# First feed-forward matrix of a decoder layer: one level of seven products against two levels

## The chip, the cores and the metric

The kernel runs on one core of one Trainium2 chip. A core has a matrix engine (TensorE, called PE, whose weight loads are listed as PEld), a vector engine (VectorE, DVE), an engine for activation functions and copies (ScalarE, ACT), a third elementwise engine (GpSimd, POOL), and SyncE (SP), whose queue issues the DMAs. TensorE writes to PSUM, in eight banks of 128 x 512 single-precision numbers; VectorE and ScalarE read PSUM, GpSimd works in SBUF alone. The metric is the device time in microseconds. Before the change the median of three runs is 2492.58 us (2489.69 to 2492.70).

## The reference

A decoder layer in float32 on x of shape (4, 2048, 512):

```
x = x + _L0_attn_ref(_layernorm(x), ...)            # a linear recurrence over the 4 leading positions
x = x + _L0_xattn_ref(_layernorm(x), ctx_1024, ...) # 16 heads, 77 context rows, softmax
x = x + _L0_ffn_ref(_layernorm(x), ...)
...
h = jnp.einsum('bsd,dh->bsh', x, W_exp) + b_exp     # 512 -> 2048
h = butterfly(h, up_weights, D_HIDDEN)
h = jax.nn.gelu(h + up_bias, approximate=False)
h = butterfly(h, down_weights, D_HIDDEN)
y = jnp.einsum('bsh,hd->bsd', h, W_con) + b_con     # 2048 -> 512
```

W_exp and the first butterfly are both linear, so they are multiplied out once into one matrix of 512 x 2048, the first feed-forward matrix; the second butterfly and W_con become one matrix of 2048 x 512.

## The kernel before

The 2048 positions are cut into 16 units of 128; a unit holds 4 x 128 = 512 rows. First the weight matrices are made (`_prepare`), which takes some 230 us and is mixed with the work of the first units. Then a loop runs over the units.

For each unit `feed_forward` does the two feed-forward products. It also takes a generator `other`, which is `front` of the next unit: layer norm, recurrence (L609), second layer norm, queries (L673), scores (L704), softmax, transposes of the weights (L725), values (L739), output matrix (L673), third layer norm. After each few matmuls of the feed-forward part, `step()` runs `front` to its next `yield`. The order of PE is thus written out by hand: a few feed-forward matmuls, a piece of the next unit's front, and so on. Some yields of `front` issue no PE work; they only let time pass until the norm's statistics and rows are ready (`normed_rows(..., wait, ...)`, 9 such yields ahead of the queries) or until the first softmax is done (4 yields). PE's queue is by hand; the queues of VectorE, ScalarE, GpSimd and SyncE are ordered by the scheduler of the framework, and every engine runs its own queue in order.

The first feed-forward matrix, 512 x 2048 against 512 rows, is done in a seven-product scheme (2 x 2 blocks, seven block products in place of eight). The sums of the left blocks were stored in DRAM as `up7` by `_prepare`; the four sums of the right blocks are made by `combine` (L808 to L811) for each unit. For each of eight output columns `p`, `up` (L838) multiplies a 128 x 128 weight block by 128 x 256 right operands, two matmuls a product, seven products, 56 calls a unit. They accumulate in three PSUM banks; one copy by ScalarE (L854) and five additions by VectorE (L857, L869, L870, L878, L881), all 128 x 256, take them out, and `gelu` (L843) is applied 128 x 256 at a time, spread over the eight columns. The weights come in DMAs of 896 KB (L1072) into a ring of three buffers.

The second matrix is done in 26 products by a list of sums (`DOWN`, `SUMS`, `_down_plan`): sums of activations by GpSimd (`made`, L891), four matmuls a product (L936), additions onto the output by VectorE (L951, L953), weights in DMAs of 512 KB (L930).

TensorE runs a float32 matmul as two records, so that two matmuls stand as four records ("x4") in the timeline.

Of the kernel before, what the change touches and what calls it, by code (L numbers as in the profile page):

```python
# [17 lines left out]
P = 128  # L18
# [7 lines left out]
ORDER = [k + j for j in range(4) for k in (0, NB // 2, NB // 4, 3 * NB // 4)]  # L26
HC = D + 1
PLACE = 2, 0, 6, 1, 3, 4, 5
# [326 lines left out]
def _prepare(nc, keep, pool, room, banks, dram, ident, wexp_t, up_low, up_high, up_bias, dn_low, dn_high, wcon,  # L355
             wup, wdn, low, bias, up7):
# [104 lines left out]
    def plain(i, c, x):  # L461
        for n in range(k):
            nc.sync.dma_start(out=up7[:, :, i, n, :].rearrange("b p q -> p b q"),
                              in_=wup[:, c + n, x : x + h].rearrange("p (b q) -> p b q", q=P))

    plain(PLACE[0], 0, 0)
    for p in range(NB // 2):
        a11, a12, a21, a22 = quarters(p)
        s = spare[:, p % 3 * 1024 : p % 3 * 1024 + 1024].rearrange("p (i k q) -> p i k q", i=4, k=k)
        nc.vector.tensor_tensor(s[:, 0], a21, a22, ALU.add)  # L470
        nc.vector.tensor_tensor(s[:, 2], a11, a21, ALU.subtract)
        nc.gpsimd.tensor_tensor(s[:, 1], s[:, 0], a11, ALU.subtract)
        nc.gpsimd.tensor_tensor(s[:, 3], a12, s[:, 1], ALU.subtract)
        nc.sync.dma_start(out=up7[p][:, 3:7], in_=s)
        if p == NB // 2 - 1:
            plain(PLACE[1], k, 0)
            plain(PLACE[3], k, h)
# [33 lines left out]
def kernel(ctx: ExitStack, tc: tile.TileContext, x, ctx_t, ssm_vec, ssm_vt, ssm_vinv, wq_t, wk_t, wv_t,  # L511
# [75 lines left out]
    def front(u, xt, res, wq=None):  # L587
# [31 lines left out]
        def normed_rows(stats, wait, by_act, last):  # L619
# [14 lines left out]
            for _ in range(wait):  # L634
                yield
# [17 lines left out]
        xnt = yield from normed_rows(second_norm, (1, 12, 9)[min(u, 2)], by_act, False)  # L653
# [66 lines left out]
        def turned(t, g):  # L720
# [6 lines left out]
            if g > 1 or not u:  # L727
                nc.scalar.copy(pt, ps[0:NK])  # L728
            else:
                nc.vector.tensor_copy(pt, ps[0:NK])  # L730
# [22 lines left out]
        for t in range(T + 1):  # L753
# [11 lines left out]
            if t == 2:  # L765
                values(0)
                values(1)
                if u == 1:
                    next_stats()
# [33 lines left out]
    def combine(xnt, res):  # L803


        b11, b12, b21, b22 = (xnt[:, c : c + 2, t : t + 2, :] for c in (0, 2) for t in (0, 2))
        t1, t2, t3, n4 = (tb[:, i].rearrange("p (k t q) -> p k t q", k=2, q=P) for i in range(4))
        nc.vector.tensor_tensor(t1, b12, b11, ALU.subtract)  # L808
        nc.gpsimd.tensor_tensor(t3, b22, b12, ALU.subtract)
        nc.vector.tensor_tensor(t2, b22, t1, ALU.subtract)  # L810
        nc.gpsimd.tensor_tensor(n4, b21, t2, ALU.subtract)  # L811
        res.append((b11, b21, b22, n4, t1, t2, t3))

    def feed_forward(u, xt, rhs, other):
# [19 lines left out]

        def up(p, i, ps, first):
            w = live[p][0][:, PLACE[i - 1]]
# [5 lines left out]
        def gelu(out, x, b):  # L842
# [310 lines left out]
```

## Time and profile before

| | |
|---|---|
| median of three runs | 2492.58 us (2489.69 to 2492.70) |
| profiled execution, its own time | 2492.85 us |
| its span, first to last instruction | 2491.1 us |
| PE busy | 2467.8 us (99%) |
| VectorE busy | 1641.2 us (66%) |
| ScalarE busy | 846.7 us (34%) |
| GpSimd busy | 991.6 us (40%) |
| DMA | 441.26 MB, mean 177 GB/s |
| one unit, from the same matmul in one to that in the next | 147.4 us |

Busy time is the union of the instructions' spans. A matmul record lasts longer than the distance to the next one, since matmuls are pipelined; what a matmul costs PE is read from the distance of starts in the timeline. In the timeline a row merges equal instructions that follow each other: start, length of the whole row, engine, line, names, count, and in brackets how long the engine was idle before and what released it. The unit's length is the distance between rows of the critical chain that recur in each unit (913.78 us and 1061.18 us).

### The profile page before, as it was taken

The numbers are of one execution on the slowest core, as the hardware profiler recorded it, in microseconds if no ns is written. First come the engines' busy times: TensorE is split into PE (matmuls) and PEld (weight loads), VectorE is DVE, ScalarE is ACT, GpSimd is POOL, SyncE is SP. The second block draws the span as 40 slices with busy tenths as digits, with TensorE's granted clock in tenths as the row PEclk, the third lists the DMA queues.
The fourth block names the chain that finished last, engine by engine and source line by source line (L and its number), as shares of the span: only waits on it lengthen the run. The fifth ranks groups of instructions, "written<-read, shape, count | busy, mean of one in ns | idle before, by whom it ended". The sixth has DMA issues, their size and how long they took to land.

```text
span 2491.1 us, 37872 instructions
## 1 busy us (share of the span) xinstructions
PE 2467.8 (99%) x14246; PEld 2139.4 (86%) x14246; DVE 1641.2 (66%) x3843; ACT 846.7 (34%) x1405; POOL 991.6 (40%) x929
## 2 busy tenths in 40 slices
PE   8999999999999999999999999999999999999999
PEld 6877888888888888888888888888888888888888
DVE  6766767576666758667675766767666675765643
ACT  4453234241333414234241423424143341513320
POOL 5534524326152342525235252433515234251534
PEclk9999999999999999999999999999999999999999
DMA  6837554626446362544636355463645646363457
GB/s 215 277 101 287 165 207 144 228 94 207 156 158 218 128 229 98 191 175 151 222 117 225 121 166 190 156 220 103 211 144 161 212 140 221 106 197 139 159 197 250
DMA packets 291427, 441.26 MB, mean 177 GB/s; under 512 B 21049, under 2 KB 247545, under 8 KB 286893
## 3 DMA queue, kind: packets, MB, share of 16 engines
q1 hardware_dynamic: 291246, 438.85, 52.8%
q8 instruction: 114, 1.87, 0.3%
q14 instruction: 67, 0.55, 0.1%
HBM read 398.30 MB, written 39.86 MB: 176 GB/s over the span
## 4 chain that ended last, share of the span: by engine, by line
PE 94%; DVE 2%; DMA 2%; POOL 0%; ACT 0%; issue 0%; SPq 0%; ACTq 0%; POOLq 0%; DVEq 0%
PE ps_a L936 13%; PE ps_b L838 13%; PE ps_b L936 9%; PE ps_a L838 9%; PE ps_c L838 9%; PE ps_w L673 8%; PE ps_q L673 7%; PE ps_c L936 7%; PE ps_sc L704 5%; PE ps_pt L725 4%; PE ps_s L609 3%; PE ps_o L739 2%; PE ps_t L639 2%; PE ps_t L600 1%; PE ps_p L444 1%; DMA arena<-in_up_low 1%
## 5 line engine op out<-in xcount | busy, mean ns | idle before, releaser
L891 POOL TENSOR_TENSOR arena<-arena 128x512 f32<-128x512 f32 x448 | 568.0, 1275 | 533.2 <-ACT arena L843 256.5
L843 ACT ACTIVATE arena<-arena,hbias 128x256 f32<-128x256 f32 x384 | 189.9, 506 | 354.5 <-DVE arena L878 228.7
L838 PE MATMUL ps_b<-arena 128*128 128x256 f32 x1128 | 289.8, 379 | 0.0
L838 PEld LDWEIGHTS ps_b<-arena 128*128 128x128 f32 x1128 | 205.4, 190 | 28.5
L936 PE MATMUL ps_a<-arena 128*128 128x256 f32 x896 | 213.9, 379 | 0.0
L660 POOL TENSOR_TENSOR tq<-tq,xnt 128x512 f32<-128x512 f32 x16 | 20.4, 1272 | 485.6 <-DVE tq L659 470.4
L697 POOL TENSOR_TENSOR pr<-pr,sm 128x616 f32<-128x616 f32 x64 | 104.7, 1636 | 248.9 <-DVE sm L696 183.5
L838 PE MATMUL ps_a<-xnt,arena 128*128 128x256 f32 x752 | 193.2, 379 | 0.0
L936 PE MATMUL ps_b<-arena 128*128 128x256 f32 x768 | 183.8, 379 | 0.0
L936 PEld LDWEIGHTS ps_a<-arena 128*128 128x128 f32 x896 | 165.5, 190 | 20.3 <-DVE xt L951 0.2
L704 PE MATMUL ps_sc<-kbd,qt 128*128 128x308 f32 x480 | 164.7, 425 | 0.6 <-DVE w L557 0.6
L936 PEld LDWEIGHTS ps_b<-arena 128*128 128x128 f32 x768 | 144.7, 190 | 19.0
L936 PE MATMUL ps_a<-w,arena 128*128 128x256 f32 x640 | 159.6, 381 | 0.0
L725 PE MATMUL ps_pt<-ident,pr 128*77 128x128 f32 x1024 | 153.3, 273 | 2.9 <-ACT pt L728 1.5
L838 PEld LDWEIGHTS ps_a<-xnt,arena 128*128 128x128 f32 x752 | 138.4, 190 | 20.2
L673 PE MATMUL ps_q<-xnt,wq 128*128 128x256 f32 x640 | 151.2, 379 | 2.3 <-DMA wq<-wq 2.3
L725 PEld LDWEIGHTS ps_pt<-ident,pr 128*77 128x77 f32 x1024 | 130.4, 148 | 26.6 <-issue 1.9
L707 DVE TENSOR_REDUCE low<-ps_sc 128x4 f32<-128x308 f32 x240 | 114.2, 476 | 52.5 <-PE ps_sc L704 46.4
L673 PEld LDWEIGHTS ps_q<-xnt,wq 128*128 128x128 f32 x640 | 121.2, 190 | 18.9 <-issue 2.7
L628 ACT ACTIVATE xn<-xt,mv,y 128x512 f32<-128x512 f32 x48 | 35.8, 808 | 298.7 <-DVE mv L563 298.7
L936 PEld LDWEIGHTS ps_a<-w,arena 128*128 128x128 f32 x640 | 118.0, 190 | 18.1 <-issue 2.8
L784 DVE TENSOR_TENSOR xt<-ps_w,xt 128x512 f32<-128x512 f32 x99 | 66.3, 688 | 101.0 <-PE ps_w L673 101.0
(225 smaller groups left out, 5035.8 us busy)
## 6 DMA issues: line engine op xcount, KB each, us to landing
arena<-dn SPq DMA_DIRECT2D x256, 512.0 KB, 4.5
w<-dn SPq DMA_DIRECT2D x160, 512.0 KB, 4.0
arena<-up SPq DMA_DIRECT2D x79, 896.0 KB, 4.5
wq<-wq SPq DMA_DIRECT2D x16, 1792.0 KB, 8.9
w<-up SPq DMA_DIRECT2D x32, 896.0 KB, 4.6
xt<-in_x SPq DMA_DIRECT2D x11, 1024.0 KB, 6.3
dn<-arena SPq DMA_DIRECT2D x8, 1152.0 KB, 6.3
out<-xt SPq DMA_DIRECT2D x33, 256.0 KB, 3.3
```

What stands on the lines that cost most here:

```text
L609: nc.tensor.matmul(ps[:, 2 * i : T, f * NS : (f + 1) * NS], lhsT=xpt[:, i, c * (P // NS) + f, :], rhs=gt[:, 0 : T - 2 * i, :], start=i == ...
L639: nc.tensor.transpose(ps[:, c, :], rows[t][:, c * P : (c + 1) * P], ident)
L673: nc.tensor.matmul(tiles[key][:, r, :], lhsT=lhs(i, r, k), rhs=rhs(i, k), start=key == i and r == 0 and k == 0, stop=k == 1, skip_group_ch ...
L697: by.tensor_tensor(pr[:, h], pr[:, h], sm[:, h].unsqueeze(2).to_broadcast([P, NH // 2, NK]), ALU.mult)
L704: nc.tensor.matmul(ps[:, 0 : 4 * NK], lhsT=qt[:, g, t, :], rhs=kbd[:, t, g, :], start=True, stop=True)
L707: nc.vector.tensor_reduce(low, sc, AX.X, ALU.min)
L725: nc.tensor.transpose(ps[0:NK, j, :], probs[t][0][:, 4 * g + j, :], ident)
L784: nc.vector.tensor_tensor(r, ps, r, ALU.add)
L838: nc.tensor.matmul(ps, lhsT=w[:, c, :], rhs=rhs[i - 1][:, c], start=first and c == 0, stop=c == 1, skip_group_check=True)
L843: nc.scalar.activation(out, x, AF.Gelu, bias=hbias[:, b : b + 1])
L891: nc.gpsimd.tensor_tensor(place(p), place(x), place(y), ALU.add if op == "+" else ALU.subtract)
L936: nc.tensor.matmul(ps, lhsT=left[:, j, :], rhs=pair[:, n, j, :], start=first and j == 0, stop=j == NB // 4 - 1, skip_group_check=True)
```

## The change

From the second unit on, each of the seven outer products of the first matrix (a 1024 x 256 left block against 256 x 256) is itself done by seven inner products. An inner product (`inner`) is four matmuls of a 128 x 128 weight block against 128 x 128, side by side in one bank of 128 x 512; there are 49 a unit. The tables `STEPS`, `PLAIN_LEFT` and `SUM_LEFT` say which outer step adds where.

- The left operands of the inner products are partly the stored outer blocks (`upo`), partly sums of them (`upi`), made once, during the first unit, by `inner_sums` on VectorE and GpSimd with DMAs in and out. The first unit itself still runs the one-level scheme (`first_up`), with its weights now read from `upo` in seven DMAs of 128 KB a column.
- The right operands of the inner products are made by `turned_right`: four 128 x 128 subtractions on GpSimd for each outer step, 28 a unit.
- Inside an outer step, products 1, 6, 7 and 4 accumulate in one bank, 2 in a second, 5 and 3 in a third. After 1, 6 and 7 the bank is copied to SBUF by ScalarE (`laid`) before the next product is accumulated onto it; VectorE adds the banks of 2, 5 and 3 to these copies (`onto`) and, for product 4, the bank to its block (`direct`). What one outer product adds to a second output block is added in SBUF by GpSimd (the last line of `onto`), 18 additions of 128 x 512 a unit. In outer step 6 `laid` is an addition by VectorE.
- Products 4 and 3 of an outer step are issued during the next one (`tail`), those of the last one after the first product of the second matrix.
- `gelu` is applied when an output block is finished (`finished`), four calls of 128 x 256 in place at a time, so after outer steps 1, 4, 5 and 6.
- The weights come in DMAs of 256 KB, four to a buffer of the same ring (`next_weight`).
- In `front`: the second norm's rows are made by ScalarE from the second unit on (before: VectorE from the third on), with 12 waiting yields in place of 9; of the transposed softmax weights, ScalarE copies three of four groups (before: two). The x of the third unit is loaded later, since its place is used by `inner_sums`.

```diff
-ORDER = [k + j for j in range(4) for k in (0, NB // 2, NB // 4, 3 * NB // 4)]
+ORDER = [k * (NB // 4) + j for j in range(4) for k in range(4)]
 HC = D + 1
-PLACE = 2, 0, 6, 1, 3, 4, 5
+STEPS = ((1, ((None, "12"),), None), (2, (("12", "11"),), "11"), (6, (("12", "21"),), None), (7, (("21", "22"),), None),
+         (4, (("22", "12"),), "12"), (5, (("22", "22"), ("21", "21")), "22"), (3, (("21", "21"),), "21"))
+PLAIN_LEFT = {1: (0, 0), 2: (1, 0), 4: (1, 1)}
+SUM_LEFT = {5: 0, 6: 1, 7: 2, 3: 3}
...
     def plain(i, c, x):
-        for n in range(k):
-            nc.sync.dma_start(out=up7[:, :, i, n, :].rearrange("b p q -> p b q"),
-                              in_=wup[:, c + n, x : x + h].rearrange("p (b q) -> p b q", q=P))
-
-    plain(PLACE[0], 0, 0)
+        nc.sync.dma_start(out=upo[i - 1], in_=wup[:, c : c + k, x : x + h])
...
-        nc.sync.dma_start(out=up7[p][:, 3:7], in_=s)
+        nc.vector.tensor_tensor(s[:, 1], a21, a11, ALU.subtract)
+        nc.vector.tensor_tensor(s[:, 3], a22, a21, ALU.subtract)
+        nc.gpsimd.tensor_tensor(s[:, 2], a22, s[:, 1], ALU.subtract)
+        nc.gpsimd.tensor_tensor(s[:, 0], a12, s[:, 2], ALU.subtract)
+        for i in range(4):
+            nc.sync.dma_start(out=upo[3 + i][:, :, p * P : (p + 1) * P], in_=s[:, i])
...
-        xnt = yield from normed_rows(second_norm, (1, 12, 9)[min(u, 2)], by_act, False)
+        xnt = yield from normed_rows(second_norm, (1, 12, 12)[min(u, 2)], u > 0, False)
...
-            if g > 1 or not u:
+            if g:
...
+            w = live[p][0][:, i - 1]
...
+        def first_up():
+            for p in range(h):
+                up_head(p)
+                if p:
+                    up_tail(p - 1)
+                up_mid(p)
+                if p < 3:
+                    _right_sums(nc.vector if p > 1 else nc.gpsimd, p + 1, wdn, rings)
+                    _right_stores(nc, p + 1, wdn, rings, dn26, (0, 1, 2))
+                    if p == 0:
+                        early.append(up_weights(4))
+                if p > 3:
+                    inner_sums(2 * p - 8)
+                    inner_sums(2 * p - 7)
+                if p >= h - 2:
+                    for n in range(4 * p - 24, 4 * p - 20):
+                        biased(n)
+            up_tail(h - 1)
+
+        def inner_sums(n):
+            i, y = STEPS[n // 2][0], slice(n % 2 * 2 * P, (n % 2 + 1) * 2 * P)
+            engine = (nc.vector, nc.gpsimd)[n % 2]
+            room = arena[:, n % 2 * 4 * D : n % 2 * 4 * D + 4 * D] if n < 8 else homes["xlast"]
+            room = room.rearrange("p (h i y) -> p h i y", h=2, y=2 * P)
+            l = room[:, 0].rearrange("p (k r) y -> p k r y", k=2)
+            o = room[:, 1]
+            for c in range(2):
+                nc.sync.dma_start(out=l[:, c], in_=upo[i - 1][:, c].rearrange("p (r y) -> p r y", r=2)[:, :, y])
+            l11, l12, l21, l22 = (l[:, c, r] for r in range(2) for c in range(2))
+            engine.tensor_tensor(o[:, 0], l21, l22, ALU.add)
+            engine.tensor_tensor(o[:, 2], l11, l21, ALU.subtract)
+            engine.tensor_tensor(o[:, 1], o[:, 0], l11, ALU.subtract)
+            engine.tensor_tensor(o[:, 3], l12, o[:, 1], ALU.subtract)
+            nc.sync.dma_start(out=upi[i - 1][:, :, y], in_=o)
+
+        def turned_right(s):
+            x, rt = rhs[STEPS[s][0] - 1], homes[f"rt{s % 3}"].rearrange("p (i q) -> p i q", i=4)
+            r11, r12, r21, r22 = (x[:, c, t] for c in range(2) for t in range(2))
+            t1, t2, t3, n4 = (rt[:, i] for i in range(4))
+            nc.gpsimd.tensor_tensor(t1, r12, r11, ALU.subtract)
+            nc.gpsimd.tensor_tensor(t2, r22, t1, ALU.subtract)
+            nc.gpsimd.tensor_tensor(t3, r22, r12, ALU.subtract)
+            nc.gpsimd.tensor_tensor(n4, r21, t2, ALU.subtract)
+            return {1: r11, 2: r21, 3: r22, 4: n4, 5: t1, 6: t2, 7: t3}
+
+        def block(o, r, t):
+            x, y = int(o[0]) - 1, int(o[1]) - 1
+            return quarter[2 * x + r][:, y + 2 * t]
+
+        order = [(s - d, j) for s in range(7) for d, j in ((0, 1), (0, 2), (1, 4), (0, 6), (1, 3), (0, 5), (0, 7)) if s >= d]
+        order += [(6, 4), (6, 3)]
+        groups = [4] * 11 + [3, 2]
+        slot = []
+
+        def next_weight():
+            if not slot:
+                n = groups.pop(0)
+                w = weights(n * 4 * P).rearrange("p (n x) -> p n x", n=n)
+                at = 49 - n - sum(groups)
+                for k, (s, j) in enumerate(order[at : at + n]):
+                    i = STEPS[s][0] - 1
+                    if j in PLAIN_LEFT:
+                        c, x = PLAIN_LEFT[j]
+                        src = upo[i][:, c, x * 4 * P : (x + 1) * 4 * P]
+                    else:
+                        src = upi[i][:, SUM_LEFT[j], :]
+                    nc.sync.dma_start(out=w[:, k], in_=src)
+                    slot.append(w[:, k])
+            return slot.pop(0)
+
+        def inner(s, j):
+            w, right = next_weight(), live[s][0][j]
+            tag = {2: "a", 5: "c", 3: "c"}.get(j, "b")
+            if j in (1, 2, 5):
+                live[s][1][tag] = bank(tag)
+            ps = live[s][1][tag]
+            for n in range(4):
+                nc.tensor.matmul(ps[:, n * P : (n + 1) * P], lhsT=w[:, n * P : (n + 1) * P], rhs=right,
+                                 start=j in (1, 2, 5) and n == 0, stop=True, skip_group_check=True)
+            step()
+            return ps.rearrange("p (j q) -> p j q", q=P)
+
+        def laid(s, ps, r, t):
+            for x, to in STEPS[s][1]:
+                if s == 6:
+                    nc.vector.tensor_tensor(block(to, r, t), ps, block(x, r, t), ALU.add)
+                    continue
+                nc.scalar.copy(raw(s, r, t), ps)
+                return
+
+        def raw(s, r, t):
+            return spare[f"x{r + t}"] if s == 5 else block(STEPS[s][1][0][1], r, t)
+
+        def onto(s, ps, r, t):
+            y = block("21", r, t) if s == 6 else raw(s, r, t)
+            nc.vector.tensor_tensor(y, ps, y, ALU.add)
+            for x, to in STEPS[s][1] if 0 < s < 6 else ():
+                nc.gpsimd.tensor_tensor(block(to, r, t), raw(s, r, t), block(x, r, t), ALU.add)
+
+        def direct(s, ps):
+            for x, to in STEPS[s][1]:
+                if x is None:
+                    nc.scalar.copy(block(to, 1, 0), ps)
+                else:
+                    nc.vector.tensor_tensor(block(to, 1, 0), ps, block(x, 1, 0), ALU.add)
+
+        def finished(s, r):
+            o = STEPS[s][2]
+            if o:
+                x, y = int(o[0]) - 1, int(o[1]) - 1
+                k = 2 * x + r
+                for n in range(4):
+                    q = quarter[k][:, y::2, n, :]
+                    gelu(q, q, 4 * k + n)
+
+        def tail(s, j):
+            ps = inner(s, j)
+            if j == 4:
+                direct(s, ps)
+                finished(s, 1)
+            else:
+                onto(s, ps, 0, 1)
+                finished(s, 0)
+
+        def later_up():
+            rights = turned_right(0)
+            for s in range(7):
+                live[s] = (rights, {})
+                laid(s, inner(s, 1), 0, 0)
+                onto(s, inner(s, 2), 0, 0)
+                if s:
+                    tail(s - 1, 4)
+                laid(s, inner(s, 6), 0, 1)
+                if s:
+                    tail(s - 1, 3)
+                if s < 6:
+                    rights = turned_right(s + 1)
+                five = inner(s, 5)
+                laid(s, inner(s, 7), 1, 1)
+                onto(s, five, 1, 1)
+                if s == 1 and u + 2 < NU:
+                    xts[u + 2] = load_x(u + 2)
+                biased(s)
+            biased(7)
...
+        if u:
+            later_up()
+        else:
+            first_up()
...
-            if rest[0] == 1:
-                up_tail(h - 1)
+            if rest[0] == 1 and u:
+                tail(6, 4)
+                tail(6, 3)
+            if not u and rest[0] < 12 and not rest[0] % 2:
+                inner_sums(8 + rest[0] // 2)
+            if not u and rest[0] == 13:
+                xts[2] = load_x(2)
...
-    up7 = dram.tile([NB // 2, P, 7, 2, P], F32, name="up7")
+    upo = dram.tile([7, P, 2, HID // 2], F32, name="upo")
+    upi = dram.tile([7, P, 4, HID // 4], F32, name="upi")
...
-        for i in ((slice(2, 5), slice(0, 2), slice(5, 7)) if p == 0 else (slice(0, 7),)):
-            nc.sync.dma_start(out=w[:, i], in_=up7[p][:, i])
+        for i in range(7):
+            nc.sync.dma_start(out=w[:, i], in_=upo[i][:, :, p * P : (p + 1) * P])
```

## Prediction

> **What bounds the kernel now.** I read the busy shares first, then the chain that ended last, then the list of waits and the timeline of one unit in the middle, since the shares do not say what a wait in one place costs.
>
> ```profile
> PE 2467.8 (99%) x14246; PEld 2139.4 (86%) x14246; DVE 1641.2 (66%) x3843; ACT 846.7 (34%) x1405; POOL 991.6 (40%) x929
> ...
> PE 94%; DVE 2%; DMA 2%; POOL 0%; ACT 0%; issue 0%; SPq 0%; ACTq 0%; POOLq 0%; DVEq 0%
> ```
>
> PE is the bound, and in the units it never waits: the longest waits of PE in the list of waits are 5.4, 2.3, 2.3 and 2.3 us, all before 233 us. So every PE microsecond removed is won, and every new PE wait is lost in full. The timeline gives the price of a matmul, by distances of starts, and the second norm's waiting stretch:
>
> ```profile
> 145.38 1.73 PE L485 MATMUL ps_p<-arena 128*128 128x128 f32 x14
> 146.95 0.39 PE L485 MATMUL ps_p<-bdd,arena 128*128 128x128 f32 x2
> ...
> 933.11 1.47 PE L609 MATMUL ps_s<-gt,xpt 128*128 128x256 f32 x8
> 934.42 1.03 PE L838 MATMUL ps_b<-arena 128*128 128x256 f32 x4
> 935.29 1.03 PE L838 MATMUL ps_c<-xnt,arena 128*128 128x256 f32 x4
> 936.15 1.03 PE L838 MATMUL ps_a<-xnt,arena 128*128 128x256 f32 x4
> 937.01 1.03 PE L838 MATMUL ps_b<-arena 128*128 128x256 f32 x4
> ```
>
> A record with 128 columns and full 128 x 128 weights costs (146.95 - 145.38) / 14 = 112 ns; eight of L485 at 109.32 to 110.21 give 111 ns. A call of `up` (four records of 256 columns) costs 0.863 us (27 calls from 2417.03 to 2440.34). In the stretch shown nothing of the front stands between the calls: there the feed-forward products alone must cover whatever they wait for. ScalarE's prices:
>
> ```profile
> 903.22 2.93 ACT L628 ACTIVATE xn<-arena,mv,y 128x512 f32<-128x512 f32 x4 [29.61 <-DVE mv L563]
> ...
> 971.29 1.28 ACT L715 ACT_TABLE_LOAD   x1
> 972.59 1.23 ACT L715 ACTIVATE pr<-pr 128x1232 f32<-128x1232 f32 x1
> 973.84 1.28 ACT L843 ACT_TABLE_LOAD   x1
> 975.13 0.51 ACT L843 ACTIVATE arena<-arena,hbias 128x256 f32<-128x256 f32 x1
> 975.54 0.35 ACT L854 COPY arena<-ps_a 128x256 f32<-128x256 f32 x1
> ...
> 987.72 0.90 ACT L843 ACTIVATE arena<-arena,hbias 128x256 f32<-128x256 f32 x2
> ```
>
> A table load holds ScalarE 1.30 us, a softmax exponential 1.25, a gelu 0.41 when others follow (0.51 alone), a norm row 0.71, a 128 x 512 copy from PSUM 0.59 (groups of L640 and L601). ScalarE runs them in order, and the exponential needs another table than the gelu.
>
> **What is saved.** Before: 56 calls a unit x 0.863 = 48.4 us. After: 49 inner products of eight records x 112 ns = 0.893 us each, 43.8 us. 4.6 us a unit, in 15 units: -69 us. The rest of PE's work is the same.
>
> **The wait in outer step 2 (A).** I name an inner product by outer step/product. PE's order there is 1/4, 2/6, 1/3, 2/5, 2/7, all in the uncovered stretch, which now holds 12 products. 2/7 accumulates onto the bank of 2/6, so it waits for ScalarE's copy of 2/6. In the built program's order of ScalarE, the same in units 2 to 14, this copy stands behind: the wait for VectorE's addition of 1/4, a table load, a gelu, two rows of the second norm, three gelus. Counted from the end of 1/4: VectorE starts 0.2 us after a product's end (921.38 to 921.58 for such a hand-over) and takes 0.69 (group of L784); the norm's small operations, some 0.2 us each, stand in its queue, so the addition ends at 1.25; load 2.55; gelu 2.95; two rows 4.4 (the statistics end at about 2.6: four of 0.65 us, then 13 small ones mixed with additions); three gelus 5.65; copy 6.25. PE has 2/6, 1/3 and 2/5 to run, 3 x 0.893 = 2.7. Wait 3.6 us. Bounds: 3.3, if VectorE has nothing ahead of the addition, and 4.8, if the mean durations of the groups (0.506, 0.806) hold instead of the overlapped ones. In the second unit there is no load at this place, 2.4. 13 x 3.6 + 2.4 = 49 us.
>
> The Trainium skill (ScalarE: Activation LUTs, What ACT_TABLE_LOAD costs) puts a switch at 2.66 us, a load of 1.28 and a drain of 1.38. The rows show the next activation 1.30 us after the load's start (971.29, 972.59), so I go by the row; by the page A would be 5.0 us and the sum 18 us higher for this term.
>
> **The wait in outer step 5 (B).** During the first softmax the front's four waiting yields leave 4/4, 5/6, 4/3, 5/5, 5/7 uncovered. 5/7 waits for the copy of 5/6, and ScalarE's order ahead of it is the exponential, a table load, four gelus. From the end of the last score matmul: VectorE's minimum and subtraction with one addition ahead 1.4 (0.48 + 0.48 + 0.2 without it: 1.2), exponential 2.65, load 3.95, gelus 5.6, copy 6.1; PE runs four products, 3.6. Wait 2.5 (2.1 to 3.0) x 14 = 35 us.
>
> **Outer step 6 (C).** Its bank additions are on VectorE: eight of 0.61 (overlapped) = 4.9 us, four scores 3.8, sums and scaling of the softmax 2.6, a copy 0.69, together 12.0, against PE's seven products 6.3, four scores 2.1, four groups of transposes 1.8, together 10.2. And ScalarE has a load, the exponential, another load and four gelus ahead of a copy that a score matmul's bank waits for. Bounds 0, if VectorE catches up while PE waits in B, and 2.7, both delays in full. I take 1.5, nearer VectorE's own excess of 1.8: 21 us.
>
> **The clock.** Idle PE has a price:
>
> ```profile
> 200.53 1.97 PE L673 MATMUL ps_q<-xnt,wq 128*128 128x256 f32 x8 [2.31 <-DMA wq<-wq]
> ...
> 232.17 1.13 PE L838 MATMUL ps_a<-xnt,w 128*128 128x256 f32 x4 [2.27 <-DMA w<-up]
> ...
> 234.00:235.00 1.00, 1.00 (x4) 0.71 (x3) 0.62 (x2) 1.00 (x1) 0.69 (x1) 0.50 0.76 317
> ```
>
> After 2.27 us of idling the granted clock is 0.50 (last row, of a table of stretches: the column after the five engines) and the calls that follow take 1.71 and 0.92 us in place of 0.86 and 0.52, until 236.7; after 2.31 us it stays 1.00. One in two, then, for some 1.7 us each. A is longer, B as long; 14 x 1.2 = 17 us, between 0 and 14 x 2 x 1.7 = 48.
>
> The Trainium skill (TensorE: Matmul & The Clock Gate, Why this matters for your kernels) speaks against this change: no idle of PE beyond about 3 us, or the clock halves. By that limit only A would pay, each time, 24 us in place of 17; the trace has one halving at 2.27 us already.
>
> **The rest.** The last unit has no front, so 0.893 us a product is all the cover there: step 2, 5 and 6 have 0.5, 2 and 2 us of gelus and GpSimd additions (1.275 us each, six in step 5) too many, plus the start of the second matrix: 6 us (2 to 10). The first unit gains nothing and makes the inner sums: 14 lots of four 128 x 256 additions (0.42 us VectorE, 0.75 GpSimd), each behind a DMA in (4.1 us to landing for 256 KB) and ahead of a DMA out, on queues that also issue its weights; the six lots in its second matrix share one room, some 8.5 us a round (landing, additions, store) against 5.5 us a pair of products (3.45 of its own and four pieces of front of 0.5 on average). 8 us (0, if hidden by the ring of three buffers, to 20). GpSimd's 18 additions (23 us) and 28 subtractions (0.40 us each by the row of L381, 11 us) a unit, and ScalarE's 19 copies (11 us), lie beside PE's 147 us; GpSimd then has 62 + 34 = 96 us of work a unit. Cover gone, their price is what A to C hold.
>
> Sum: -69 + 49 + 35 + 21 + 17 + 6 + 8 = +67. The profiled execution took 2492.85 us, its span 2491.1; it lies 0.3 us from the median. Prediction 2560 us. All terms low: -69 + 45 + 29 + 2 = +7; all high: -69 + 67 + 42 + 38 + 48 + 10 + 20 = +156. Its own range is 2505 to 2635 us.
>
> **Rivals.**
> 1. The saving stays: ScalarE's copy is in time. ScalarE is busy 34% and PE lost under 3 us to it before. Against it: the copies had the length of four products then, now three (A) or four short ones (B), and in-order queues put loads and gelus ahead. It decides at A + B + C = 4.6 us a unit; with no waits but first and last unit, 2493 - 69 + 14 = 2438 us.
> 2. The two cancel: waits of 4.6 us a unit, about 2493 us. A and B at their lower ends are 5.4.
> 3. Weights come late. In the uncovered stretch 256 KB are wanted every 0.893 us, 294 GB/s. The windows from 923 to 929 us show 385 and 399 GB/s, but those around 908 to 923 us only 262 to 305. Twelve products at 262 GB/s take 12.0 in place of 10.7 us; +1.3 us a unit on top of the rest, and with a backlog of x (1 MB) and wq (1.8 MB) ahead of them up to 5: 2580 to 2650 us.
> 4. The scheme does not save: if a record with 128 columns cost its weight load (190 ns, groups of PEld), an inner product would cost 1.52 us and the units 15 x (74.5 - 48.4) = 390 us more, 2880 us. The L485 rows speak against it.
>
> **How the numbers follow.** A measurement tells about 0.2% (5 us) from no change. Forecast 0.80; rival 1: 0.08; rival 2: 0.03; rival 3 or a pile-up of C and the clock beyond 2635: 0.08; rival 4: 0.01. Leaving out rival 1 and the upper tail, the range is 2500 to 2635 us. Faster 0.08, same 0.03, slower 0.89.
>
> **What would show it.** PE busy falls to some 95%. The waits list PE L973 <- ACT L983 some 28 times, 14 of 3 to 5 us and 14 of 2 to 3. A unit is about 152 us long, not 143. Dips of the granted clock recur once or twice a unit. An L973 row of four matmuls is 0.89 us from the next in the covered part. ScalarE's rows show load, gelu, two L630, three gelus, copy. I am wrong if PE L973 waits for ScalarE under 2 us a time, or mostly for DMA or GpSimd.

## The result, and the profile after

The changed kernel takes 2667.22 us (median of 4, 2664.99 to 2668.89) against 2492.03 us; the ratio is 1.0704 with a 95% interval from 1.0686 to 1.0723. The forecast had the sign right and the size wrong: +67 us was said, +175 us came. The profiled execution has a span of 2664.6 us.

The busy shares and the shares of the chain, the two lines that answer to those shown of before:

```profile
PE 2479.4 (93%) x16766; PEld 2223.3 (83%) x16766; DVE 1696.7 (64%) x3638; ACT 983.5 (37%) x1654; POOL 1545.6 (58%) x1647
...
PE 72%; DVE 13%; ACT 6%; DMA 3%; POOL 3%; issue 2%; SPq 1%; DVEq 0%; POOLq 0%; ACTq 0%
```

PE is busy for 2479 us, 12 us more than before, although less matrix work is left. That alone says that part of its work ran slower. The list of PE's waits (total, times, longest):

```profile
PE ps_b L973 <- ACT arena L983: 112.7, 29, 5.6
PE ps_sc L708 <- ACT pt L732: 15.3, 14, 1.1
```

The waits are the forecast ones, with ScalarE's copy as their end, 29 times: two in each of the fourteen units from the second on, and one in the last. None of these fifteen units waits for a DMA. The timeline of one unit around the second norm, which answers to the rows at 933 to 937 us of before, shows where A (the wait before 2/7) comes from. Columns are start, duration, engine, line, operation, and the idle time in brackets:

```profile
1327.51 1.26 POOL L993 TENSOR_TENSOR arena<-arena 128x512 f32<-128x512 f32 x1 [0.83 <-DVE vi L554]
1327.54 1.26 DVE L555 TENSOR_SCALAR y<-vi 128x4 int32<-128x4 int32 x1
1327.70 1.95 PE L973 MATMUL ps_b<-arena 128*128 128x128 f32 x16
...
1330.16 1.27 POOL L993 TENSOR_TENSOR arena<-arena 128x512 f32<-128x512 f32 x1 [0.70 <-DVE w L559]
1330.18 1.26 DVE L560 SCALAR_TENSOR_TENSOR y<-w,y 128x4 f32<-128x4 f32 x1
...
1331.37 0.68 DVE L1000 TENSOR_TENSOR arena<-ps_b,arena 128x512 f32<-128x512 f32 x1
...
1332.12 1.28 ACT L838 ACT_TABLE_LOAD   x1 [4.47 <-DVE w L558]
...
1333.42 0.51 ACT L838 ACTIVATE arena<-arena,hbias 128x256 f32<-128x256 f32 x1
1333.83 1.50 ACT L630 ACTIVATE xn<-arena,mv,y 128x512 f32<-128x512 f32 x2
...
1335.24 1.29 ACT L838 ACTIVATE arena<-arena,hbias 128x256 f32<-128x256 f32 x3
...
1336.44 0.56 ACT L983 COPY arena<-ps_b 128x512 f32<-128x512 f32 x1
...
1337.05 3.78 PE L973 MATMUL ps_b<-arena 128*128 128x128 f32 x16 [5.61 <-ACT arena L983]
```

Load, gelu, two norm rows, three gelus, copy: ScalarE's chain is the forecast one, element for element, and takes from 1332.12 to 1337.0. But its start is late. Product 1/4 ends at about 1328.6 (half of the first row), and VectorE adds it only at 1331.37, 2.8 us later, where 0.2 and a few small operations were reckoned. Ahead of it in VectorE's queue two 128 x 4 operations (L555 and L560) took 1.26 us each. Each began within 0.03 us of a GpSimd addition of 1.26 or 1.27 us and ended with it. Such an operation took 0.16 us elsewhere. (The bracket of the table load names L558, which ended 0.01 us before it; the gelu behind the load reads what the addition wrote.)

The table of stretches shows what follows the wait (the last column but two is the granted clock):

```profile
1334.40:1335.20 0.80, 0.00 (x0) 0.00 (x0) 0.00 (x0) 0.80 (x2) 0.80 (x2) 1.00 0.29 110
1335.20:1336.00 0.80, 0.00 (x0) 0.00 (x0) 0.00 (x0) 0.80 (x3) 0.72 (x3) 0.66 0.07 26
...
1341.60:1342.40 0.80, 0.80 (x6) 0.80 (x6) 0.00 (x0) 0.80 (x2) 0.80 (x2) 0.57 0.51 105
1342.40:1343.20 0.80, 0.80 (x10) 0.80 (x9) 0.62 (x1) 0.66 (x2) 0.10 (x1) 1.00 0.60 189
```

The clock is halved from 1335.5 to 1342.3: 6.8 us, two stretches of 3.41 and not one. PE works in it from 1337.05, so 2.6 us are lost after a wait of 5.6 us. B (the wait before 5/7) is in the same unit:

```profile
1374.64 1.71 ACT L838 ACTIVATE arena<-arena,hbias 128x256 f32<-128x256 f32 x4
...
1376.26 0.56 ACT L983 COPY arena<-ps_b 128x512 f32<-128x512 f32 x1
...
1376.87 1.16 PE L973 MATMUL ps_b<-arena 128*128 128x128 f32 x8 [2.41 <-ACT arena L983]
```

To see where all of the time is, each PE matmul was charged from its start to the next one's (at most its own duration), and what fell into a stretch of halved clock was split into the work at full clock and the loss. The 14 units are those from the first L973 row (367 us) to the last unit's (2564 us), before: of L838 from 331 to 2395 us.

| us | first unit | one of the 14 units | first matrix in it | other PE work | idle | lost to half clock | last unit |
|---|---|---|---|---|---|---|---|
| before | 149.2 | 147.4 | 48.5 | 98.9 | 0.0 | 0.0 | 96.5 |
| after | 184.3 | 156.9 | 44.3 | 99.5 | 9.25 | 3.85 | 101.0 |

So 133 us come from the fourteen units, 35 from the first and 4.5 from the last; 1 us from the time before them.

### The profile page after: what moved, and what is told of

It is laid out like the page before. It is cut to its first block, busy times and chain, and to the rows that moved or that the text cites. A ratio compares the mean times of both kernels' runs of the same rounds, so it can differ in the third digit from the quotient of the medians.

```text
span 2664.6 us, 45385 instructions
## 1 busy us (share of the span) xinstructions
PE 2479.4 (93%) x16766; PEld 2223.3 (83%) x16766; DVE 1696.7 (64%) x3638; ACT 983.5 (37%) x1654; POOL 1545.6 (58%) x1647
## 4 chain that ended last, share of the span: by engine, by line
PE 72%; DVE 13%; ACT 6%; DMA 3%; POOL 3%; issue 2%; SPq 1%; DVEq 0%; POOLq 0%; ACTq 0%
PE ps_a L1073 11%; PE ps_b L973 10%; PE ps_b L1073 8%; PE ps_q L677 7%; PE ps_w L677 7%; PE ps_c L1073 6%; PE ps_sc L708 4%; PE ps_pt L729 3%; PE ps_c L973 3%; ACT arena L838 3%; PE ps_s L611 3%; PE ps_a L973 3%; DVE arena L991 2%; PE ps_o L743 2%; PE ps_t L643 2%
## 5 line engine op out<-in xcount | busy, mean ns | idle before, releaser
L846 POOL TENSOR_TENSOR arena<-arena 128x512 f32<-128x512 f32 x448 | 571.2, 1284 | 252.3 <-PE ps_c L1073 190.2
L993 POOL TENSOR_TENSOR arena<-arena 128x512 f32<-128x512 f32 x270 | 340.9, 1270 | 313.4 <-DVE arena L991 277.9
L973 PE MATMUL ps_b<-arena 128*128 128x128 f32 x2000 | 284.6, 292 | 77.0 <-ACT arena L983 76.6
L973 PEld LDWEIGHTS ps_b<-arena 128*128 128x128 f32 x2000 | 271.2, 207 | 92.3 <-ACT arena L983 80.2
L983 ACT COPY arena<-ps_b 128x512 f32<-128x512 f32 x270 | 157.3, 582 | 376.4 <-PE ps_b L973 376.3
L991 DVE TENSOR_TENSOR arena<-ps_c,arena 128x512 f32<-128x512 f32 x210 | 143.6, 684 | 219.2 <-ACT arena L983 168.3
L838 ACT ACTIVATE arena<-arena,hbias 128x256 f32<-128x256 f32 x504 | 216.2, 497 | 142.1 <-DVE arena L1000 80.4
L1073 PE MATMUL ps_a<-arena 128*128 128x256 f32 x1016 | 246.5, 384 | 6.7 <-DVE xt L1088 3.6
L973 PE MATMUL ps_b<-arena,w 128*128 128x128 f32 x1000 | 141.9, 291 | 36.9 <-ACT arena L983 36.1
L1073 PE MATMUL ps_b<-arena 128*128 128x256 f32 x688 | 172.7, 381 | 0.0
L973 PEld LDWEIGHTS ps_b<-arena,w 128*128 128x128 f32 x1000 | 134.5, 206 | 44.2 <-ACT arena L983 38.0
L732 ACT COPY pt<-ps_pt 77x512 f32<-77x512 f32 x192 | 107.9, 576 | 117.1 <-PE ps_pt L729 116.9
L1073 PEld LDWEIGHTS ps_b<-arena 128*128 128x128 f32 x688 | 126.3, 191 | 16.3
```

Source lines behind the costliest of these rows:

```text
L838: nc.scalar.activation(out, x, AF.Gelu, bias=hbias[:, b : b + 1])
L846: nc.gpsimd.tensor_tensor(place(p), place(x), place(y), ALU.add if op == "+" else ALU.subtract)
L973: nc.tensor.matmul(ps[:, n * P : (n + 1) * P], lhsT=w[:, n * P : (n + 1) * P], rhs=right, start=j in (1, 2, 5) and n == 0, stop=True, skip ...
L983: nc.scalar.copy(raw(s, r, t), ps)
L991: nc.vector.tensor_tensor(y, ps, y, ALU.add)
L993: nc.gpsimd.tensor_tensor(block(to, r, t), raw(s, r, t), block(x, r, t), ALU.add)
```

## The experiments

The same charging is used below; "unit" is the mean of the fourteen. Five of the kernels were run once (the second to the sixth below); the four runs of the changed kernel lie within 4 us.

**Work put into the waits.**

```
-                five = inner(s, 5)
+                five = inner(s, 5, {2: 6, 5: 3}.get(s, 1))
...
-            for n in range(4):
+            for n in [*range(4)] * times:
```

> Redundant work put into the two waits: inner product 2/5 is computed six times and 5/5 three times (each time from the start of its bank, so the result is that of the last), 4.5 and 1.8 us of TensorE work a unit more. Theory of the clock: the stretches at half clock, 54 us of lost TensorE work over the fourteen units (by the rows' own durations and the granted clock), come from the idling alone, and the waits for ScalarE's copies end when they did. So the waits shrink from 5.6 and 2.4 to about 1.1 and 0.6 us, the half clock leaves the units, and the time FALLS by about 50, to 2610 to 2625 us, though 88 us of work are added. Rival, the half clock has another cause (load on the chip): the time stays at 2660 to 2670. Second rival, the waits are not for ScalarE but for what TensorE itself does later (weights, banks): the added work comes on top, 2720 to 2755.

Measured: 2649.2 us, 1.0632 (1.0614 to 1.0649) of before, so 18 us less than the changed kernel with 88 us of added work in the fourteen units. That is the forecast way, but outside the forecast of 2610 to 2625. One unit, and the longest entry of the wait list:

```profile
1321.77 5.52 PE L973 MATMUL ps_c<-arena 128*128 128x128 f32 x48
1328.45 2.05 PE L973 MATMUL ps_b<-arena 128*128 128x128 f32 x16 [1.15 <-ACT arena L983]
...
PE ps_pt L729 <- ACT pt L732: 39.7, 18, 2.5
```

The waits shrank to 1.15 and 0.6 us, and the loss to half clock from 3.85 to 0.85 us a unit, 42 us. That is the theory of the clock, and both rivals are out: the waits end when ScalarE ends, and with less idling the halved clock goes too. But 17 us of it came back: in step 6 PE idles for 2.5 us a unit in place of some 1.3. There the scheduler had put a copy of turned probabilities behind a second load and two gelus, so the wait that was called C got longer. The forecast of 50 us had not reckoned with a change in ScalarE's order.

**GpSimd's additions taken out of the stretch.**

```
-            for x, to in STEPS[s][1] if 0 < s < 6 else ():
+            for x, to in STEPS[s][1] if 2 < s < 6 else ():
```

> GpSimd's outer additions of outer steps 1 and 2 are left out (six of 1.27 us a unit; the first matrix's outer combination is then incomplete). Theory of the port: the operations of the second norm's statistics on VectorE that took 1.26 instead of 0.16 us ended together with one of these GpSimd additions and were held by it; without them VectorE's addition of product 1/4 starts about 2 us sooner, the wait before 2/7 falls from 5.6 to 3.3 to 3.8 us, and the time to 2615 to 2640 us (2.0 us of waiting and some 1 us of half clock, times 13 or 14). Rival, VectorE is late by its own queue: the wait stays over 5 us and the time over 2655.

Measured: 2599.79 us; the wait before 2/7 fell from 5.6 to 2.7 us. Time and wait both fell by more than forecast.

```profile
1455.87 1.95 PE L973 MATMUL ps_b<-arena,w 128*128 128x128 f32 x16
...
1456.93 0.16 DVE L560 SCALAR_TENSOR_TENSOR y<-w,y 128x4 f32<-128x4 f32 x1
1457.01 0.68 DVE L1000 TENSOR_TENSOR arena<-ps_b,arena 128x512 f32<-128x512 f32 x1
...
1462.27 1.94 PE L973 MATMUL ps_b<-arena 128*128 128x128 f32 x15 [2.66 <-ACT arena L983]
```

The small operation is back at 0.16 us, and VectorE's addition starts 0.25 us after the product's end (1455.87 and 0.89), 2.5 us sooner than in the changed kernel. The other 0.4 us come from the table load, which here runs before the addition (1.3 us won) while the norm's rows wait 0.8 us for their statistics. The same operation of the norm in three kernels, least, median and longest ns (changed, before, without the additions):

```profile
L555 DVE TENSOR_SCALAR y<-vi x48: 160/1190/1266, 26.9 to 2553.0; 128x4 int32<-128x4 int32 x48
```

```profile
L553 DVE TENSOR_SCALAR y<-vi x48: 153/160/179, 27.2 to 2374.8; 128x4 int32<-128x4 int32 x48
```

```profile
L555 DVE TENSOR_SCALAR y<-vi x48: 161/170/1284, 26.7 to 2488.1; 128x4 int32<-128x4 int32 x48
```

So GpSimd's additions hold the norm's small operations on VectorE, which have two inputs in SBUF (L560) or one (L555). They do not hold everything that works in SBUF alone: the sums of the softmax (L699, one input of 128 x 616) took 781 to 796 ns in all 128 cases of the changed kernel. In the kernel before, other small operations of this chain were held now and then as well (its L558 took 0.16 us as a rule and 1.19 at most). VectorE's additions that read PSUM are not held: one of them takes 0.69 us at 1378.93 in the changed kernel, in the middle of two GpSimd additions (1378.57 to 1381.20). The Trainium skill (SBUF — State Buffer, SBUF: two separate sides) says this: VectorE and GpSimd share one port pair by an exclusive lock, which a VectorE operation needs if it has two SBUF inputs or runs in a two-port mode, and the loser waits for the whole instruction. The rows agree for two inputs, with 1.26 for 0.16 us in L560. L555 has one input, and no run here shows in which mode it runs. The prediction had not looked there.

**The gelus after the copies.**

```
                 direct(s, ps)
-                finished(s, 1)
+                if s == 6:
+                    finished(s, 1)
...
                 onto(s, five, 1, 1)
+                if s:
+                    finished(s - 1, 1)
+                    finished(s - 1, 0)
```

> The gelus of outer steps 1, 4 and 5 are issued after the last copy of the following step instead of right after their products; the scheduler then puts ScalarE's copy of 5/6 ahead of the table load and the gelus, and the copy of 2/6 ahead of three of four gelus, but still behind a load, a gelu and two rows of the norm. Theory of ScalarE's queue: the wait before 5/7 goes from 2.4 to under 0.5 us, the one before 2/7 from 5.6 to 4.2 to 4.8, and with half of the halved clock gone the time is 2570 to 2610 us. Rival, 5/7 waits for something else that ends at the same time (weights, VectorE): it still waits 2 us or more, time over 2640. Second rival, the delayed gelus come back as a wait in step 6 or in the second matrix: 2/7 and 5/7 as said, but 1 to 3 us of new waits a unit, 2610 to 2645.

Measured: 2571.02 us, 96 us less than the changed kernel with the same work.

```profile
PE ps_b L973 <- ACT arena L983: 59.6, 15, 4.4
PE ps_pt L729 <- ACT pt L732: 13.1, 18, 1.9
```

15 waits instead of 29: B is gone, A is 4.4 us, both as said. A unit takes 150.1 us, with 4.85 us idle and 1.5 lost to half clock. The order in ScalarE's queue is the cause of B, and of 1.2 us of A. Nothing came back in step 6; there too the wait got shorter.

**The side edits alone, in the kernel before.** (Its `normed_rows(..., (1, 12, 12)[...], u > 0, False)`, `if g:` ahead of ScalarE's copy of the turned probabilities, and the place of `next_stats` for the third unit, as in the change.)

> The kernel before, with the change's edits to the front alone: twelve waiting yields before the second norm's rows in every unit, those rows on ScalarE in all later units, three of four copies of the turned probabilities on ScalarE, and the statistics of the third unit's first norm made later. Theory: TensorE covers all of it as it did, 2485 to 2500 us. Rival, part of the 9.7 us a unit comes from these side edits and not from the two levels: 1 us a unit or more, over 2506 us.

Measured: 2522.22 us. The theory was wrong here, and the rival right in size: a unit takes 148.6 us, 1.2 more than before, with 0.84 us idle, and the first unit 157 us, 8 more.

```profile
PE ps_o L741 <- ACT pt L730: 9.2, 14, 0.7
PE ps_pt L727 <- ACT pt L730: 6.0, 5, 2.0
```

PE waits for ScalarE's copies of the turned probabilities, of which the edits give ScalarE a third; that this one alone makes them late was not tried in the old scheme. The front's edits together, which the prediction had costed at nothing apart from the two rows of the norm, cost 30 us in the old scheme.

**That copy given back to VectorE, in the changed kernel.**

```
-            if g:
+            if g > 1 or not u:
```

> One side edit undone: in the later units two of four copies of the turned probabilities go to VectorE again, as before. Alone in the old scheme the side edits made a unit 1.2 us longer, with 0.7 us of TensorE waiting for such a copy before the attention's sums. Theory: the wait of step 6 (1.1 us before a score matmul, 0.3 before a transpose) comes from ScalarE's queue and shrinks by about 1 us a unit, time 2645 to 2657. Rival, VectorE, with 4.9 us of additions in that step, is the one that is late: the copies on VectorE make the wait longer, 2667 to 2690.

Measured: 2670.53 us, no gain; the 3 us more lie in the first unit (188.9 us in place of 184.3).

```profile
PE ps_b L973 <- ACT arena L983: 111.9, 29, 5.6
PE ps_b L973 <- DVE arena L981: 8.3, 14, 0.6
```

The wait for ScalarE in step 6 is gone from the list, one of 0.6 us for VectorE has taken its place, and a unit idles for 8.5 us in place of 9.25. But the loss to half clock rose from 3.85 to 4.55 us a unit. Neither theory holds: each of the two engines makes a wait in step 6, and what little was gained, the clock took.

**No inner sums.**

```
         def inner_sums(n):
+            return
...
-                    if j in PLAIN_LEFT:
-                        c, x = PLAIN_LEFT[j]
+                    if True:
+                        c, x = PLAIN_LEFT.get(j, (0, 1))
```

> The inner sums of the weights are not made: the first unit loads, adds and stores nothing for them, and from the second unit on all 49 inner products take plain quarter blocks of the same size in their place (so the first matrix is not computed rightly from there on). The units from the second on have the same instructions and the same bytes. Theory: of the 36 us by which the first unit grew (182 to 367 us against 182 to 331), the inner sums cost 20 to 32, by holding VectorE and GpSimd for their loads and by their transfers; the time is 2635 to 2650 us. Rival, the weights of the first unit are late because the first matrix now lies in pieces of 512 bytes a row: the first unit stays over 170 us and the time over 2652.

Measured: 2643.6 us; the first unit takes 162.0 instead of 184.3 us and the fourteen units are unchanged (156.9). So 22 of the 35 us are the sums. Some 8 of the other 13 are the side edits, if they cost here what they cost alone. What the last 5 are was not tried.

**ScalarE's queue in PE's order.** The gelus of step 1 are issued two at a time behind the copies of steps 3 and 4, those of 4 and 5 as above, the first two norm rows behind the copy of 2/7, and the copies of the turned probabilities as before the change.

```
             for n in range(wait):
...
                 yield
+                if late and n == wait - 2:
+                    row(0)
+                    row(1)
...
+        def ease():
+            for q, b in due[:2]:
+                tc.keep_in_program_order(nc.scalar.activation(q, q, AF.Gelu, bias=hbias[:, b : b + 1]))
+            del due[:2]
...
                 laid(s, inner(s, 7), 1, 1)
+                ease()
                 onto(s, five, 1, 1)
+                if s == 2:
+                    due.extend(finishing(1))
```

> ScalarE's queue put in the order in which TensorE needs it: the gelus of outer step 1 are issued two at a time behind the copies of steps 3 and 4, those of steps 4 and 5 after the last copy of the next step, the second norm's first rows behind the copy of 2/7, and the copies of the turned probabilities are shared as before. The same instructions, but one table load or so. Theory (all of A and B is ScalarE's order, the half clock follows from the idling): 2/7 and 5/7 wait under 0.5 us, the units take 144.5 to 146 us in place of 156.9, the first unit keeps its 36 us: 2485 to 2515 us. Rival: the waits move to the next consumer of a late thing (the rows of the norm, held by VectorE's statistics, or the copy of 2/7): 1.5 to 4 us a unit are left, 2520 to 2570 us.

Measured: 2507.87 us, 1.0065 (1.0048 to 1.0082) of before. A unit takes 144.86 us: 1.2 us idle, nothing lost to half clock, 2.5 us less than before the change. The same stretch of the timeline, and the longest entry of PE's wait list (L980 is the inner product, L990 ScalarE's copy, L988 VectorE's addition in step 6):

```profile
1266.97 1.97 PE L980 MATMUL ps_b<-arena 128*128 128x128 f32 x16
...
1268.07 0.59 ACT L990 COPY arena<-ps_b 128x512 f32<-128x512 f32 x1 [2.09 <-PE ps_b L980]
...
1269.07 1.52 ACT L630 ACTIVATE xn<-arena,mv,y 128x512 f32<-128x512 f32 x2 [0.41 <-DVE mv L565]
...
PE ps_b L980 <- DVE arena L988: 15.4, 14, 1.1
```

2/7 (the first eight records of the first row) starts without a wait, its copy follows 0.2 us after its end, and the norm's rows come after it. GpSimd's additions are all there and VectorE's operations are held as before (the addition of 1/4 starts at 1267.06, 2.8 us after that product's end), but A is gone: the late VectorE did harm only because ScalarE's queue waited for it in order. The theory holds. Against the kernel before, 16 us of loss remain: the fourteen units win 36 us, but the first unit takes 190 us, 41 more, the last 4.7 more, and the time ahead of the first unit 3 more.

**A version that beats both: three edits on top of that.** The inner sums are made in place, in four rooms instead of two; their loads, additions and stores are issued one pair of products apart; and the last unit, which has no front to fill its waits, uses one level again.

```
-        if u:
+        if 0 < u < NU - 1:
             later_up()
...
+                if not u and p > 4:
+                    sums_store(p - 5)
                 up_head(p)
...
+                if not u and p > 2:
+                    sums_load(p - 3)
                 up_mid(p)
...
+                if p > 3:
+                    sums_add(p - 4)
```

> On top of the reordered ScalarE queue: the inner sums of the weights are made in place (half the room, so four rooms instead of two), and their loads, additions and stores are issued at three different places, each one pair of products after the one before, so that SyncE's queue, VectorE and GpSimd no longer stand waiting for a landing, an addition or a store while weights are queued behind them; the last unit, which has no front beside its products, computes its first matrix with one level as before. Theory: the 20 to 25 us that the sums cost the first unit are in-order waiting and not bytes or additions; the first unit falls from 190 to 155 to 168 us, the last from 101 to 96.5, the units keep 144.9: 2465 to 2485 us, under the kernel before. Rival: the transfers themselves (14 MB more through the same queues) make the first unit's weights late: it stays at 175 us or more, and the time at 2490 or more.

Measured: 2486.68 us, 0.9978 (0.9969 to 0.9987) of before: faster than both kernels, than the old one by 0.2%, which is little, but the interval leaves out 1. The first unit takes 174.7 us, just under the rival's 175 and above the theory's 155 to 168; the last takes 99.5 us where 96.5 were expected. The timeline around its longest wait (SPq is SyncE's queue):

```profile
242.43 1.99 SPq L952 DMA_DIRECT2D upi<-arena  x2
244.47 5.08 SPq L1268 DMA_DIRECT2D w<-upo  x7
247.98 2.07 PE L862 MATMUL ps_a<-xnt,w 128*128 128x256 f32 x4 [10.23 <-DMA w<-upo]
```

The weights (L1268) stand in the queue behind two stores (L952) that wait for their additions.

**The same with the sums' DMAs on ScalarE's queue** (`nc.scalar.dma_start` for their loads and stores).

> The same as the kernel before this one (reordered ScalarE queue, sums in place and in three stages, last unit with one level), but the loads and stores of the inner sums are issued from ScalarE's queue instead of SyncE's. There one wait of 10.2 us of TensorE for a piece of weights was left in the first unit: in SyncE's queue the piece stood behind two stores that waited for their additions until 242.4 us. Theory: with the stores on another queue the piece comes in time, the wait of 10 us falls to under 3 us and the time by 6 to 14 us, to 2472 to 2481 us. Rival: ScalarE, which then stands waiting for the same additions, is late with its gelus and copies, and TensorE waits for those instead: 2484 to 2500 us.

Measured: 2500.61 us, 1.0042 (1.0028 to 1.0055) of before. The wait of 10.2 us for weights fell to 0.6, and the rival came true: first unit 185.6 us.

```profile
244.12 4.00 ACTq L952 DMA_DIRECT2D upi<-arena  x2
248.22 0.38 ACT L872 COPY arena<-ps_a 128x256 f32<-128x256 f32 x1 [3.65 <-DMA upi<-arena]
```

A copy out of one of PE's banks waits 3.65 us behind two stores. **Started one pair later on SyncE's queue:**

> Loads and stores of the inner sums are on SyncE's queue again; the whole chain of loads, additions and stores starts one pair of products later, when GpSimd and VectorE are through with the sums of the second matrix. Theory: the wait of 10.2 us in the first unit came from the first stores, whose additions GpSimd did only after its sums for the second matrix; started later, they no longer hold the weights queued behind them: first unit 163 to 170 us in place of 174.7, time 2474 to 2483 us. Rival: the sums that are pushed back make the second matrix of the first unit late by as much: 2484 to 2492 us.

Measured: 2489.75 us, 0.9992 (0.9983 to 1.0001) of before; first unit 177.3 us. The wait for weights is 3.1 us, and in the second matrix 11.4 us have come up:

```profile
PE ps_b L1123 <- POOL arena L946: 11.4, 1, 11.4
```

The rival again: the sums put off are in GpSimd's way later. In the three arrangements some 10 us of waiting were not removed but moved: to weights, to results of VectorE (7.3 and 4.1 us the longest, with ScalarE held by the DMAs it issues), to sums of GpSimd. How to place the sums without them stays open.

## Why the prediction was wrong in size

By its own terms, in us over the whole kernel:

| step | forecast | measured | from |
|---|---|---|---|
| saving | -69 | -62 | 14 x 4.2 and 3.7 in the last unit |
| A | +49 | +77 | 13 x 5.6 and 4.4 |
| B | +35 | +34 | 14 x 2.4 |
| C | +21 | +19 | 129.5 idle in the units, less A and B |
| the clock in the units | +17 | +54 | 14 x 3.85 |
| last unit | +6 | +8 | 5.9 idle, 1.7 half clock |
| first unit and inner sums | +8 | +35 | 184.3 - 149.2 |
| other PE work | 0 | +8 | 14 x 0.6 |
| sum | +67 | +173 | spans: 2664.6 - 2491.1 = 173.5 |

Right were the sign and its mechanism, B, C in size, the price of an inner product (113 ns a record where 112 and 111 were read), the last unit, and what was said would show it: 28 waits of L973 for L983 (29), PE busy 93%, ScalarE's rows in the named order. Rivals 1 (the saving stays), 2, 3 (weights late) and 4 (a record costs its weight load) are out: the units idle for ScalarE and for no DMA, and at full clock the products take 44.3 us. Of the signs, the unit of 152 us and the two classes of waits (3 to 5 and 2 to 3 us) failed on the sizes of A and of the clock: 157 us and 5.6.

Four terms failed.

- **The clock**, the largest, 37 us short. The step was "one in two, then, for some 1.7 us each", read from two waits before. (By these words two waits a unit make 1.7 us and 24 us in all; the 1.2 of the sum has no working.) A halves the clock every time, and for two stretches, since the work done at half clock in the first one is too little to end it (1.6 of its 3.41 us are idle in the unit shown). B halves it in ten of fourteen units, by its place on the clock's grid. The upper bound given, 48 us, fell short too. Work put into the waits took most of it away. The rule of the Trainium skill (TensorE: Matmul & The Clock Gate, Why this matters for your kernels), which the prediction weighed, gave 24 us for A alone, and was nearer; A alone cost 14 x 2.6 = 36 us.
- **A**, 28 us short, above its bound of 4.8. The step was "the addition ends at 1.25". The additions that the change gives to GpSimd hold two of VectorE's small operations ahead of it, so it ends at 3.4. The prediction had costed GpSimd's 18 additions as lying beside PE's time; it asked what they take from GpSimd and not what they take from VectorE. Leaving six out of them gave 2.9 us back.
- **The first unit**, 27 us short, above its bound of 20. The sums were reckoned as engine time and rounds of DMA. 22 us are the sums, by the experiment without them. 15 us went when they were made in four rooms and issued in stages (190.0 to 174.7), and some 10 us of waiting then moved from queue to queue. That these 15 were queues standing in order fits the rows, but rooms and stages were not tried apart. Some 8 us are side edits, if these add up.
- **Small ones**: 0.6 us a unit of other PE work and 0.3 of products. Score matmuls went from 259 to 264 ns a record, second-matrix ones from 217 to 219; why was not tried. C had the right size, but its main term was VectorE's additions, and PE's longest wait there is the 1.1 us for ScalarE's copy of the turned probabilities; the side edits alone make 1.2 us a unit more in the old scheme, 0.7 of it such a wait. Two slips of the range changed little: its lower end stands as 2505 and as 2500, and A's upper end is 65 us by its own bounds, not 67.

## What to carry to other kernels

Where a copy that the bottleneck engine waits for goes to an engine with an in-order queue, put that queue in the bottleneck's order before judging the scheme: here the same instructions, but for 56 copies that went from ScalarE to VectorE, gave 2667 and 2508 us. Price an idle of TensorE with the halved clock behind it, and price work moved to GpSimd also by what it holds on VectorE. One-time preparation inside the first unit has to be priced by the queues that it blocks, not by its operations.

## What the runs showed of the hardware

- **The clock's rule is sharp.** The halved stretches lie on a grid of 3.413 us that does not follow the kernel. Over eleven traces (the two kernels and the first nine experiments; the first 60 us or so of each left out), each stretch of that grid was sorted by PE's idle time in it and by the clock of the next one. At full clock some 7670 stretches kept it, none of them with more than 1.97 us idle, and 163 were followed by half clock, all but two with 1.97 us or more (the two: 1.74 and 1.87). At half clock the next one was half again with 0.67 us idle or more (64) and full with 0.57 or less (163). Both say nearly the same: under some 1.4 us of work, counted at full clock, in 3.41 us, the next stretch runs at half (3.41 - 1.97 = 1.44; half of 3.41 - 0.67 and of 3.41 - 0.57 is 1.37 and 1.42). The two exceptions are not explained. So a wait of 2.4 us costs nothing or 1.7 us, depending on where it falls on the grid, which is why ten of the fourteen B waits, all of 2.4 us, halve the clock and four do not, and why an edit that only shifts a wait can win or lose by the clock. The Trainium skill (TensorE: Matmul & The Clock Gate, What's actually happening) has the free-running window of 3413 ns; that a window must be idle for the clock to fall, as it says, is not so here, where waits of 2.4 us halve it.
- **Issuing a DMA takes its queue's time.** A piece of weights in seven DMAs held SyncE's queue for 5.08 us in the row above, 0.7 us each. Four loads of the sums held ScalarE's for 3.6 us (at 229.61 in the version with ScalarE's queue), while no activation ran.
